# Inputs of the next pair made during the scan: two state-space layers and two token layers on one core

## The chip, the core and the metric

The kernel runs on one core of a Trainium2 chip. A core has five engines that run beside each other, each through its own list of instructions in order: TensorE (PE in the profile, with its weight loads as PEld), VectorE (DVE), ScalarE (ACT), GpSimd (POOL) and SyncE (SP, which here issues the DMA transfers). They wait for each other by semaphores. Operands lie in SBUF, results of TensorE in the eight banks of PSUM. The metric is the device time in microseconds (us) from start to end of the program.

## What is computed

The input x is four images of 64 x 64 places with 96 channels. Two layers of a two-dimensional selective scan follow each other, then two layers of linear attention and a quantised feed-forward net on the tokens. Of a scan layer, the part that matters here is

```
x   = x + layer(groupnorm(x))
xz  = einsum('bhwc,ec->bhwe', x, in_proj_w)          # 96 -> 2 * 192
xp, z = split(xz, 2)
xc  = silu(depthwise 3 x 3 convolution of xp + conv_b)
xs  = xc in four orders: rows, columns, and both from the end
x_dbl -> dts, B, C                                    # 6 + 16 + 16 rows
delta = softplus(dts @ dt_projs_w + bias)
h_t = exp(delta_t * A) * h_(t-1) + delta_t * u_t * B_t   # 16 states a channel
y_t = sum over states of C_t * h_t,  + D * u_t
y   = layernorm(sum of the four orders) * silu(z)
out = einsum('bhwd,cd->bhwc', y, out_proj_w)
```

## The kernel before

Two images make a pair, so there are four units in the order layer 0 pair 0, layer 0 pair 1, layer 1 pair 0, layer 1 pair 1. The 192 channels of a pair's two images fill three tiles of 128 rows: tile 0 and 1 hold 128 channels of one image each, tile 2 the remaining 64 of both. `u[0..2]` hold the inputs of the scan, 128 x 4096 each, in SBUF.

For each unit `between_scans` (L107) runs a stage, and then `scan.run()` the scan. The stage interleaves two generators: `scan_outputs` (L249) of the unit before, and `scan_inputs` (L122) of the unit to come. `scan_inputs` measures the group norm (`measure`, L174), projects 512 places at a time into padded images in SBUF (`project`, L198), writes silu(z) to DRAM (`zg`), and convolves: `conv_product` (L147) by nine matrix products with diagonal weights on TensorE, `conv_chain` (L158) by nine multiply-adds on VectorE. Here the order on an engine is the scheduler's. `scan_outputs` works in 16 groups of 256 places: load `zt`, `xr` and the sums `ys`; layer norm, transposition, product with `zt`, projection `po`, addition and store.

The scan (`PairScan.scan`, L458) is written out by hand: `InOrder` (L56) keeps the compute engines to the order of the program. Its 48 steps are (direction k, chunk of 1024 places, tile j), and a step is eight groups of two states, named by `n0`, the first of the two. For each state VectorE runs a first-order recurrence over 1024 places (`h`). Its two inputs are da = exp(delta A) from ScalarE and b = delta u B. The strings `OWN` and `SHARED` (L45) say who makes b for each state: V is VectorE, from B spread by TensorE with a selector `sel`; A is ScalarE (`outer`, L512) and a transposition by TensorE; G is GpSimd (`start_dbu`, L541). The result or its factor stands in `bp`, of which there are two. GpSimd multiplies h by C (`cb`, spread by DMA from DRAM); three groups later (LAG) TensorE turns the product to time order and adds it up in `yp`. `bp` takes four banks, `yp` two; `m0` and `m1` of one bank each serve two further pieces of work: `discretise` (L421), which makes delta, du and dut of the step to come, and `project` (L375), which makes B, C and dt of the chunk to come. Both are generators that `drive` (L481) takes on at named places; a value after `yield` is the n0 (for `project` with the tile or half ahead of it) at which the next part is to be issued.

After the last scan `token_layers` (L860) takes the outputs of the last unit together with the attention of the first images.

Of the kernel before, what the change touches and what calls it, by code (L numbers as in the profile page):

```python
# [44 lines left out]
OWN, SHARED = "VAVAVAAGVAVAVAVA", "VGVAVAVGVAVGVAVV"  # L45
# [39 lines left out]
class ScanLayer:  # L85


    def __init__(self, tc, pw, dram, x_src, w, n):
# [5 lines left out]

        self.zg = [dram.tile([3, 128, L], F32, name=f"zg{n}{pr}") for pr in range(NB // 2)]
# [11 lines left out]
def between_scans(tc, cst, ident, half, u, before, scan, after):  # L107


    with ExitStack() as stage:  # L110
        ins = scan_inputs(tc, stage, cst, ident, half, u, scan, *after)
        if before is not None:
            pp = stage.enter_context(tc.tile_pool(name="c_ps", bufs=2, space=PSUM))
            outs = scan_outputs(tc, stage, ident, half, *before, pp)
            for _ in outs:
                for _ in range(2):
                    next(ins, None)
        for _ in ins:
            pass


def scan_inputs(tc, stage, cst, ident, half, u, scan, layer, pr):  # L122


    nc = tc.nc
    par, zg, x_src = layer.par, layer.zg[pr], layer.x_src
    pa = stage.enter_context(tc.tile_pool(name="a", bufs=1))
    p2 = stage.enter_context(tc.tile_pool(name="a2", bufs=3))
    pp = stage.enter_context(tc.tile_pool(name="a_ps", bufs=5, space=PSUM))

    wi = pa.tile([C, 2, 2 * DI], F32, name="wi")
    nc.sync.dma_start(out=wi, in_=layer.w["wi"].rearrange("i c d -> c i d"))

    diag = pa.tile([128, 9, 128], F32, name="diag")
    for tap in range(9):
        nc.gpsimd.tensor_scalar(diag[:, tap], ident, par[:, 0, P_CONV + tap : P_CONV + tap + 1], None, ALU.mult)

    imgs = []
    for j in range(3):
        img = pa.tile([128, HW + 2, HW + 2], F32, name=f"img{j}", tag=f"img{j}")  # L140
        nc.gpsimd.memset(img[:, 0], 0.0)
        nc.gpsimd.memset(img[:, HW + 1], 0.0)
        nc.gpsimd.memset(img[:, 1 : HW + 1, 0:1], 0.0)
        nc.gpsimd.memset(img[:, 1 : HW + 1, HW + 1 : HW + 2], 0.0)
        imgs.append(img)

    def conv_product(j, c):  # L147

        ps = pp.tile([128, 8, HW], F32, name="cps", tag="mm")
        for tap in range(9):  # L150
            dy, dx = divmod(tap, 3)
            v = imgs[j][:, c + dy : c + dy + 8, dx : dx + HW]
            nc.tensor.matmul(ps, diag[:, tap], v, start=(tap == 0), stop=(tap == 8))
        nc.scalar.activation(
            u[j][:, HW * c : HW * (c + 8)], ps.rearrange("p h w -> p (h w)"), AF.Silu, bias=par[:, 0, P_CB : P_CB + 1]
        )

    def conv_chain(j, c):  # L158

        s, cols = j // 2, slice(HW * c, HW * (c + 16))  # L160
        to = u[j][:, cols].rearrange("p (h w) -> p h w", w=HW)
        for tap in range(9):
            dy, dx = divmod(tap, 3)
            v = imgs[j][:, c + dy : c + dy + 16, dx : dx + HW]
            weight = par[:, s, P_CONV + tap : P_CONV + tap + 1]
            if tap == 0:
                nc.vector.tensor_scalar(to, v, weight, par[:, s, P_CB : P_CB + 1], ALU.mult, ALU.add)
            else:
                nc.vector.scalar_tensor_tensor(to, v, weight, to, ALU.mult, ALU.add)
        nc.scalar.activation(u[j][:, cols], u[j][:, cols], AF.Silu)  # L170

    norms = []

    def measure(i):  # L174

        stats = p2.tile([C, 8, 6], F32, name="stats")
        for g in range(8):
            xt = p2.tile([C, 512], F32, name="xt", bufs=4)
            nc.sync.dma_start(out=xt, in_=x_src[2 * pr + i, :, 512 * g : 512 * g + 512])
            nc.vector.bn_stats(stats[:, g], xt)  # L180
            if g % 2:
                yield
        mv = p2.tile([C, 2], F32, name="mv")
        nc.vector.bn_aggr(mv, stats.rearrange("c g s -> c (g s)"))

        gm = pp.tile([C, 1], F32, name="gm", tag="mm")
        nc.tensor.matmul(gm, cst["group"], mv[:, 0:1], start=True, stop=True)
        mean = p2.tile([C, 1], F32, name="mean")
        nc.vector.tensor_copy(mean, gm)
        dev = p2.tile([C, 1], F32, name="dev")  # L190
        nc.vector.tensor_tensor(dev, mv[:, 0:1], mean, ALU.subtract)
        spread = p2.tile([C, 1], F32, name="spread")
        nc.vector.scalar_tensor_tensor(spread, dev, dev, mv[:, 1:2], ALU.mult, ALU.add)
        gv = pp.tile([C, 1], F32, name="gv", tag="mm")
        nc.tensor.matmul(gv, cst["group"], spread, start=True, stop=True)
        norms.append((mean, rstd_of(nc, p2, gv, [C, 1], "gn", half[:C, 0:1])))

    def project(i, c):  # L198


        mine, other = slice(D1 * i, D1 * i + D1), slice(D1 - D1 * i, 128 - D1 * i)
        cols, rows = slice(512 * c, 512 * c + 512), slice(1 + 8 * c, 9 + 8 * c)
        xn = p2.tile([C, 512], F32, name="xn")
        nc.sync.dma_start(out=xn, in_=x_src[2 * pr + i, :, cols])
        nc.vector.tensor_scalar(xn, xn, *norms[i], ALU.subtract, ALU.mult)
        pss = []
        for q in range(3):
            ps = pp.tile([128, 8, HW], F32, name=f"ips{q}", tag="mm")
            nc.tensor.matmul(ps, wi[:, i, 128 * q : 128 * q + 128], xn, start=True, stop=True)
            pss.append(ps)  # L210
        nc.scalar.copy(imgs[i][:, rows, 1 : HW + 1], pss[0])
        nc.scalar.copy(imgs[2][mine, rows, 1 : HW + 1], pss[1][mine])
        zs = p2.tile([128, 2, 512], F32, name="zs", bufs=2)
        flat = [ps.rearrange("p h w -> p (h w)") for ps in pss]
        nc.scalar.activation(zs[other, 0], flat[1][other], AF.Silu)
        nc.scalar.activation(zs[:, 1], flat[2], AF.Silu)
        nc.sync.dma_start(out=zg[i, :, cols], in_=zs[:, 1])
        nc.sync.dma_start(out=zg[2, mine, cols], in_=zs[other, 0])

    for i in range(2):  # L220
        yield from measure(i)
    for c in range(8):
        project(0, c)
        if c % 2:
            yield

    for c in range(8):
        project(1, c)
        if c == 2:
            conv_chain(0, 0)  # L230
        elif c == 5:
            conv_chain(2, 0)
        if c % 2:
            yield
    conv_product(1, 0)
    conv_product(1, 8)
    beginnings = scan.begin(nc, pp)
    for n in range(2, 8):
        conv_product(*((1, 8 * n) if n < 6 else (0, 8 * n)))
        for _ in range(4):  # L240
            next(beginnings, None)
        yield
        conv_chain(*((0, 16), (0, 32), (2, 16), (2, 32), (2, 48), (1, 48))[n - 2])
        yield
    for _ in beginnings:
        pass


def scan_outputs(tc, stage, ident, half, layer, pr, pp, turned="pt", summed="po"):  # L249
# [3 lines left out]
    p2 = stage.enter_context(tc.tile_pool(name="c2", bufs=3 if layer.last and pr else 2))  # L253
# [3 lines left out]
    for g in range(NT // 2):  # L257
# [25 lines left out]
        for t in range(2):  # L283
            for i in range(2):
                cols = slice(DI * i, DI * i + DI)
                nc.scalar.activation(
                    ys[:, t, cols], ys[:, t, cols], AF.Identity, bias=shift[:, t, i : i + 1], scale=rs[:, t, i : i + 1]
                )

        gt = p2.tile([128, 3, 2, 128], F32, name="gt")  # L290
        for t in range(2):
            pt = pp.tile([128, 3, 128], F32, name="pt", tag=turned)
            for j, first in enumerate((0, 256, 128)):
                nc.tensor.transpose(pt[:, j], ys[:, t, first : first + 128], ident)
            for s, js in ((0, slice(0, 2)), (1, slice(2, 3))):
                nc.scalar.activation(
                    gt[:, js, t],
                    pt[:, js],
                    AF.Identity,
                    bias=par[:, s, P_NB : P_NB + 1],  # L300
                    scale=par[:, s, P_NW : P_NW + 1],
                )
        nc.vector.tensor_tensor(gt, gt, zt.rearrange("p j (t q) -> p j t q", q=128), ALU.mult)
# [37 lines left out]
class PairScan:  # L341
# [112 lines left out]
    def run(self):  # L454
        with ExitStack() as stage:
            self.scan(stage, InOrder(self.tc))
# [495 lines left out]
def constants():  # L952
# [6 lines left out]
    for n in range(NS):  # L959
        for i in range(2):  # L960
            sel[:, i, n, n, i] = 1
# [101 lines left out]
```

## Time and profile before

| what | us |
|---|---|
| median of three runs | 10648.89 |
| lowest and highest | 10646.76, 10650.05 |
| the profiled execution | 10664.13 |
| its span | 10662.4 |
| the four scans, first to last VectorE scan operation | 2295.4, 2295.8, 2293.4, 2300.3 |
| from start to the first scan | 151.2 |
| from scan to scan | 226.7, 225.6, 237.8 |
| from the last scan to the end | 635.7 |

The page of the profile gives for each engine its busy time, then the span in 40 slices with the busy share of each in tenths, and groups of like instructions: line and engine, what is written and read, how many, then busy time, mean of one in ns, and the idle time of the engine just ahead of them with what ended it. Instructions that the scan issues all have the line of the helper (L71), so they are told apart by the names of their tiles. A product of two float32 operands shows as two passes on PE.

### The profile page before, as it was taken

To read this page: it belongs to the slowest core of one execution; us is meant where nothing else is said; L and a number is where in the kernel's file an instruction comes from. 1 tells how busy PE (TensorE), PEld (TensorE's weight loads), DVE (VectorE), ACT (ScalarE), POOL (GpSimd) and SP (SyncE) were. 2 spreads that over 40 slices of the span, in tenths; PEclk is the share of its full clock that TensorE was granted. 3 is DMA by queue.
4 is the path that set the end of the run, shared out by engine and by line. 5 is a ranking of instruction groups with operands and counts; after the bars stand their busy time and mean duration, and the time that the engine had idled before them with its cause. 6 is when DMAs were issued, how large, how long until landed. Compare 5 with 4: busy or idle time off the path is not lost. (4 is left out here: it accounts for less than half of the span.)

```text
span 10662.4 us, 142477 instructions
## 1 busy us (share of the span) xinstructions
PE 8056.0 (76%) x47648; PEld 5958.1 (56%) x47648; DVE 9606.8 (90%) x6874; ACT 8773.7 (82%) x18779; POOL 9021.4 (85%) x5298
## 2 busy tenths in 40 slices
PE   7777777777777777776877777777777777777666
PEld 4555555554555555554455555555455555555554
DVE  8999999997999999998899999999699999999755
ACT  6888888885888888886788888888598888888666
POOL 4999999992899999996599999999299999999645
PEclk9888898988888898998989889898888889899887
DMA  4677777775677777777567777777577777777710
GB/s 146 208 212 217 218 220 218 219 219 156 203 213 212 218 220 220 217 219 206 162 209 215 213 219 221 221 217 219 147 207 210 207 219 218 219 217 220 198 34 24
DMA packets 908758, 2126.70 MB, mean 199 GB/s; under 512 B 331094, under 2 KB 640664, under 8 KB 710296
## 3 DMA queue, kind: packets, MB, share of 16 engines
q1 hardware_dynamic: 908024, 2117.59, 69.3%
q8 instruction: 378, 6.19, 0.3%
q14 instruction: 356, 2.92, 0.1%
HBM read 1955.85 MB, written 161.48 MB: 199 GB/s over the span
## 5 line engine op out<-in xcount | busy, mean ns | idle before, releaser
L71 POOL TENSOR_TENSOR h<-h,cb 128x1024 f32<-128x1024 f32 x3072 | 7198.3, 2367 | 236.1 <-issue 68.6
L71 DVE TENSOR_TENSOR_SCAN h<-da,last,bp 128x1024 f32<-128x1024 f32 x2064 | 4736.5, 2335 | 142.0 <-PE bp L71 21.9
L71 ACT ACTIVATE x<-dut,bt 128x128 f32<-128x128 f32 x12288 | 3509.7, 378 | 1.6 <-PE bp L71 1.5
L71 PE MATMUL yp<-ident,h 128*128 128x128 f32 x24576 | 3365.5, 297 | 10.9 <-POOL h L71 10.9
L71 PEld LDWEIGHTS yp<-ident,h 128*128 128x128 f32 x24576 | 3191.8, 157 | 126.0 <-issue 74.0
L71 ACT ACTIVATE da<-delta,amat 128x1024 f32<-128x1024 f32 x2752 | 3076.3, 1147 | 95.7 <-DVE h L71 94.6
L71 PE MATMUL bp<-ident,x 128*128 128x128 f32 x10240 | 1672.5, 315 | 1292.8 <-DVE h L71 949.4
L71 PEld LDWEIGHTS bp<-ident,x 128*128 128x128 f32 x10240 | 1353.6, 162 | 1856.2 <-ACT x L71 1011.7
L71 DVE TENSOR_TENSOR bp<-du,bp 128x1024 f32<-128x1024 f32 x1472 | 1780.9, 1214 | 271.4 <-PE bp L71 269.6
L71 DVE TENSOR_TENSOR_SCAN h<-da,bp 128x1024 f32<-128x1024 f32 x688 | 1537.7, 2275 | 53.7 <-ACT da L71 12.9
L71 PE MATMUL bp<-bparts,sel 96*128 96x512 bf16 x2944 | 923.1, 399 | 755.2 <-DVE h L71 736.2
L71 PEld LDWEIGHTS <-sel 96*128 96x128 bf16 x2944 | 226.9, 100 | 1551.1 <-DVE h L71 1032.5
L71 ACT ACTIVATE bp<-delta,amat 128x1024 f32<-128x1024 f32 x320 | 358.2, 1119 | 520.1 <-DVE h L71 518.6
L71 POOL TENSOR_TENSOR dbu<-du,bb 128x1024 f32<-128x1024 f32 x320 | 755.4, 2361 | 0.0
L71 POOL COPY last<-h 128x2 f32<-128x2 f32 x1152 | 218.5, 190 | 490.0 <-DVE h L71 487.8
L71 DVE TENSOR_TENSOR_SCAN h<-bp,last,dbu 128x1024 f32<-128x1024 f32 x240 | 558.8, 2329 | 18.2 <-POOL dbu L71 17.1
L81 POOL TENSOR_TENSOR ln_rs<-ln_ve,half 128x4 f32<-128x4 f32 x64 | 84.8, 1325 | 546.6 <-DVE ln_ve L79 452.2
L71 PE MATMUL xps<-u,wx 128*76 128x512 f32 x720 | 532.7, 825 | 0.0
L71 ACT ACT_TABLE_LOAD x380 | 487.5, 1283 | 25.1 <-DMA x<-xo 18.3
L71 POOL TENSOR_TENSOR du<-delta,u 128x1024 f32<-128x1024 f32 x188 | 497.1, 2644 | 0.0
L71 PE MATMUL dps<-cdt,wdt 12*128 12x512 f32 x752 | 434.7, 658 | 0.0
L71 ACT COPY ysum<-yp 128x1024 f32<-128x1024 f32 x192 | 194.4, 1013 | 289.9 <-PE yp L71 289.8
(156 smaller groups left out, 6339.7 us busy)
## 6 DMA issues: line engine op xcount, KB each, us to landing
cb<-crow SPq DMA_DIRECT2D x1024, 1024.0 KB
cb<-crow SPq DMA_DIRECT2D x1024, 512.0 KB
bb<-crow SPq DMA_DIRECT2D x384, 256.0 KB
bb<-crow SPq DMA_DIRECT2D x128, 512.0 KB
y<-ysum SPq DMA_DIRECT2D x192, 256.0 KB
kept<-y SPq DMA_DIRECT2D x160, 256.0 KB
y<-ysum SPq DMA_DIRECT2D x64, 512.0 KB
zt<-zg SPq DMA_DIRECT2D x64, 384.0 KB
```

The lines of the kernel that those rows point to most:

```text
L71: return self.tc.keep_in_program_order(getattr(self.engine, op)(*args, **kwargs))
L81: nc.gpsimd.tensor_tensor(rs, ve, half, ALU.pow)
```

## The change

The inputs of the next unit are made while a scan runs. `first_inputs` is the old `scan_inputs` for the first unit alone, with eight PSUM banks, and it also measures the norm of images 2 and 3. For the later units an object `InputsAhead` holds a list of small jobs. A projection job is one product of 128 x 512; a convolution piece of 128 x 512 is two jobs, of five and four taps, and its input is read back from DRAM (`xi`). Each job writes the bank `m0` or `m1` between the uses by `discretise` and `project`; ScalarE copies the result out two states later, and SyncE stores it (`xi`, `zg` or `conv`). Projections, norms and convolutions no longer touch `u`.

The stage between then loads `conv` into `u`, applies silu there (`take`), and runs `scan_outputs`. z is stored without silu, which `scan_outputs` applies to `zt`; `scan_outputs` also takes the statistics for the norm of the next layer from what it has just made, and half of the layer norm's scaling moves to VectorE, except in the last unit. `discretise` is issued earlier. To make room in SBUF the selector shrinks to an identity that is read with stride 0 (`both` holds it written out for tile 2), GpSimd's b is written over its input, and the skip shares a buffer with `kept`. One G in `SHARED` moves from state 11 to state 13.

```
-OWN, SHARED = "VAVAVAAGVAVAVAVA", "VGVAVAVGVAVGVAVV"
+OWN, SHARED = "VAVAVAAGVAVAVAVA", "VGVAVAVGVAVAVGVV"
...
+class InputsAhead:
...
+        projections = [[("in", i, c, q) for q in range(3)] for i in range(2) for c in range(8)]
+        conv = [[[("conv", j, c, h) for h in range(2)] for c in range(8)] for j in range(3)]
+        pieces = projections[:8] + conv[0] + projections[8:] + conv[1] + [[("diag",)]] + conv[2]
...
+    def load(self, nc, n):
...
+        self.given[n] = given = self.pb.tile([128, 10 * HW], F32, name="given", bufs=2)
...
+            nc.sync.dma_start(out=to, in_=self.layer.xi[self.pr][i, :, HW * lo : HW * hi])
...
+    def prepare(self, nc, n):
...
+            nc.scalar.activation(xn, xn, AF.Identity, bias=shift, scale=scale)
...
+    def start(self, nc, pm, tag, more):
...
+        kind, i, c, part = job
+        if kind == "conv" and part == 0 and not more:
+            return
+        self.jobs.pop(0)
+        if part == 0:
+            self.load(nc, n + 1)
...
+            ps = pm.tile([128, 512], F32, name="aps", tag=tag)
+            nc.tensor.matmul(ps, self.wi[:, 128 * part : 128 * part + 128], self.given[n][:C, :512], start=True, stop=True)
...
+            def close():
+                out = self.pb.tile([128, 512], F32, name="bout", bufs=2)
+                nc.scalar.copy(out, ps)
...
+        if part == 0:
+            self.open = pm.tile([128, 8, HW], F32, name="bps", tag=tag)
...
+        taps = (4, 0, 1, 2, 3, 5, 6, 7, 8)
+        for tap in taps[:5] if part == 0 else taps[5:]:
...
+            nc.tensor.matmul(ps[:, h, w], self.diag[:, tap], v, start=(tap == 4), stop=(tap == 8))
...
+        def close():
+            out = self.pb.tile([128, 512], F32, name="bout", bufs=2)
...
+            nc.scalar.activation(out, ps.rearrange("p h w -> p (h w)"), AF.Identity, bias=bias)
+            nc.sync.dma_start(out=layer.conv[pr][i, :, 512 * c : 512 * c + 512], in_=out)
+            self.prepare(nc, n + 1)
...
+def between_scans(tc, cst, ident, half, pn, u, before, scan, layer, pr):
...
+        def take(n):
+            for j in range(3):
+                cols = slice(T * n, T * n + T)
+                nc.sync.dma_start(out=u[j][:, cols], in_=layer.conv[pr][j, :, cols])
+                nc.scalar.activation(u[j][:, cols], u[j][:, cols], AF.Silu)
+
+        take(0)
+        outs = scan_outputs(tc, stage, cst, ident, half, pn, *before, pp)
+        beginnings = scan.begin(nc, pb)
+        for g, _ in enumerate(outs):
+            if g % 4 == 1 and g > 4:
+                take(g // 4)
...
+                if alone and i:
+                    nc.vector.tensor_scalar(v, v, scale, bias, ALU.mult, ALU.add)
+                else:
+                    nc.scalar.activation(v, v, AF.Identity, bias=bias, scale=scale)
...
+        nc.scalar.activation(zt, zt, AF.Silu)
         nc.vector.tensor_tensor(gt, gt, zt.rearrange("p j (t q) -> p j t q", q=128), ALU.mult)
...
+            for i in range(2):
+                norms[i].take(nc, xo[:, i])
...
+        yield 0
         for hf, cols in enumerate(halves):
-            yield 2 * hf
             ps = pm.tile([128, 512], F32, name="dps", tag=tags[hf])
...
-        yield 4
+        yield 2
         for ps, cols in zip(pss, halves):
             nc.scalar.activation(delta[:, cols], ps, AF.Softplus, bias=bias)
-        yield 6
+        yield 4
...
-            yield 10 + 2 * hf
+            yield 6 + 2 * hf
...
-            yield 12 + 2 * hf
+            yield 8 + 2 * hf
...
-                    out[i] = p2.tile([128, T], F32, name="dbu", bufs=1)
-                    nc.gpsimd.tensor_tensor(out[i], made[groups[g][0]][1], bbs.pop((g, i))[:, 0], ALU.mult)
+                    out[i] = bbs.pop((g, i))[:, 0]
+                    nc.gpsimd.tensor_tensor(out[i], made[groups[g][0]][1], out[i], ALU.mult)
...
+        def drive_ahead(place):
+
+            j, n0 = place
+            if later is None:
+                return
+            if n0 in (4, 6, 12, 14):
+                later.finish()
+            if n0 in (10, 12) or j < 2 and n0 in (2, 4):
+                later.start(nc, pm, "m0" if n0 >= 10 else "m1", n0 in (2, 10))
```

`drive_ahead` is called once a group: at n0 = 14 right after `drive(projecting)` ahead of the next group's inputs, and in the other groups after `drive(discretising)` and ahead of `drive(projecting)`.

## The prediction

> **What bounds the kernel now.** I read the page first, for the engines' shares, then busy time by stage, then the waits of one scan, then a timeline of a few microseconds, then the costliest groups between two scans.
>
> ```profile
> span 10662.4 us, 142477 instructions
> PE 8056.0 (76%) x47648; PEld 5958.1 (56%) x47648; DVE 9606.8 (90%) x6874; ACT 8773.7 (82%) x18779; POOL 9021.4 (85%) x5298
> ...
> DVE  8999999997999999998899999999699999999755
> ...
> 151.20:2446.60 2295.40, 1748.38 (x10646) 1326.04 (x10646) 2173.62 (x1150) 1989.59 (x4270) 2153.42 (x1197) 0.89 0.75 215
> 2446.60:2673.40 226.80, 176.24 (x530) 88.13 (x530) 155.76 (x312) 116.97 (x225) 33.13 (x41) 0.88 0.53 146
> ```
>
> The last two rows are a scan and the stage after it (columns: window, length, PE, PEld, DVE, ACT, POOL busy, clock, DMA share, GB/s). A scan fills 2173.6 of its 2295.4 us on DVE and 2153.4 on POOL: only 122 us of DVE idle are to be had there, and whatever makes DVE wait lengthens the kernel. The stages between last scan operation and first of the next take 226.7, 225.6 and 237.8 us, 690 together, with no engine full: PE 176, DVE 156.
>
> What makes DVE wait in a scan (us, times, longest):
>
> ```profile
> DVE bp L71 <- PE bp L71: 56.8, 73, 1.7
> ...
> PE dups L71 <- ACT dut L71: 19.8, 27, 1.5
> ```
>
> PE, though 76% busy, is what DVE waits for. A timeline of two groups shows why:
>
> ```profile
> 1044.37 1.21 DVE L71 TENSOR_TENSOR bp<-du,bp 128x1024 f32<-128x1024 f32 x1
> ...
> 1045.50 1.91 PE L71 MATMUL yp<-ident,h 128*128 128x128 f32 x16
> 1047.24 0.60 PE L71 MATMUL dups<-ident,du 128*128 128x128 f32 x4
> 1047.68 1.88 PE L71 MATMUL xps<-u,wx 128*76 128x512 f32 x2
> 1049.38 0.61 PE L71 MATMUL bp<-bparts,sel 96*128 96x512 bf16 x2
> 1050.18 1.21 DVE L71 TENSOR_TENSOR bp<-du,bp 128x1024 f32<-128x1024 f32 x1
> ...
> 1054.44 0.66 PE L71 MATMUL dups<-ident,du 128*128 128x128 f32 x4 [1.22 <-ACT dut L71]
> 1054.93 1.88 PE L71 MATMUL xps<-u,wx 128*76 128x512 f32 x2
> 1056.63 0.61 PE L71 MATMUL bp<-bparts,sel 96*128 96x512 bf16 x2
> ```
>
> A group takes DVE 5.8 us (one product 1.21, two scans 4.6). Both `bp` buffers are in use, so PE can't run ahead. After DVE begins a group, PE is done with `bp` and `yp` at 1047.41, 3.0 us in; the next `bp` must start about 5.0 us in. So 2.0 us of a group are free on PE. In the first group `dups` and `xps` (2.3 us) just fit: DVE goes on at 1050.18, 5.81 later. In the second PE also waited 1.22 us for ACT, and the next `bp` came at 1056.63, 6.45 in: DVE lost 1.18 us.
>
> **The skill.** "Perfetto Trace Analysis", Optimization Strategy, says that regimes with different limits may gain from being interleaved, which fits the two window rows; its Identifying the Most-Contended Engine warns that PE's busy time is no measure of PE's room, and the timeline agrees: 2.0 us a group, not 24%, and only at one place. "ScalarE: Activation LUTs", What ACT_TABLE_LOAD costs, gives 1283 ns for a load; the page here has the same mean, 1283. "DMA: Bandwidth & Descriptors", Measured, has 341 GB/s for 1 MB transfers; the trace moves 215 in a scan, with 331094 packets under 512 B, so I use the trace's.
>
> **Part 1: the stage between.** Removed: `project`, convolution and the norm's first pass. In their place 12 loads of ready convolutions and 12 Silu of 128x1024. What stays per group of outputs is little to compute and much to move: `zt` 0.39 MB, `xr` 0.20, `ys` 0.39, `xo` 0.20, 1.17 in all; 16 groups 18.7 MB, with `u` 6.3 MB: 25 MB. At 215 GB/s 116 us. DVE for a group:
>
> ```profile
> L278 DVE BATCH_NORM_STATS2 ystats<-ys 128x6 f32<-128x192 f32 x64 | 20.1, 342 | 17.2 <-DMA ys<-y 17.2
> L303 DVE TENSOR_TENSOR gt<-gt,zt 128x768 f32<-128x768 f32 x16 | 15.3, 954 | 11.6 <-ACT gt L296 11.6
> L312 DVE TENSOR_TENSOR xo<-xr,po 96x512 f32<-96x512 f32 x16 | 10.8, 678 | 13.9 <-PE po L310 13.9
> ```
>
> (instructions, busy, mean ns, idle before). 20.1+10.0 (aggregates)+15.3+10.8+5.2 (small ones), plus the two normalising products that move over from ACT (2x16 at about 0.3) and 32 statistics of `xo` (about 0.4): 84 us. ACT: 15.2+32.8 us of its present work, 16 Silu of 128x768 (0.9 by the 1.06 of 128x1024) and 12.7 for `u`: 75. So DMA is next in line, not an engine. The first `ystats` ran 16.4 us after the last scan operation (sum, store, load) and a group lasts 12 us from there. 16.4 + 15 groups at 6.6-7 + 12 + 4 to the first scan operation = 133 us; 120 if transfers are quicker, 150 if they stay as in the tail, where 16 groups take 7.7 us each. Gain 690 - 3x133 = 291 us.
>
> **Part 2: jobs in the first three scans.** Each scan gets 48 projection jobs and 24 convolution pieces, a piece cut into 5 and 4 taps in successive slots. The prices stand in the stage between: 144 passes of `cps` 64.1 us, two passes a tap, so 0.89 a tap; 96 passes of `ips` 45.3, 0.94 a projection. One stage has 216 taps and 48 projections: 216x0.89 + 48x0.94 = 237 us more for PE, from 1748 to 1985 of 2295: that fits on average and not in place. A piece is 4.45 and then 3.56 us against 2.0 free. The slots are the groups that begin with state 2, 4, 10 or 12 for tiles 0 and 1, and 10 or 12 for tile 2. In 10 and 12 of tiles 0 and 1 PE has `xps` behind the job, 1.5 us on average (180 passes 133.3). DVE then loses 2.45+1.55 = 4.0 us a piece in 2,4 and 3.95+3.05 = 7.0 in 10,12; in tile 2 4.0, of which POOL's backlog there (its own 49.4 us of a 49.9 us step) hides about 1. Mix 2:2:1: 5.0 a piece, 120 us a scan. ACT's part: in the group of state 10 the bank m0 is given free by the copy of `dut`, at 2 the bank m1 by the softplus, and PE stands behind these as in the second group above: 1.2 us on 14 pieces, 17 us. Projections fit except beside `xps` or behind ACT: 0.5 on average, 24 us. Some of this falls where DVE waits already (122 us a scan): minus 20. Sum 140 a scan, 420. Bounds: 84 (3.5 a piece, nothing else) to 200 (ACT late at every slot).
>
> ACT gains 48x0.59 + 24x0.6 + 16x0.5 = 51 us of 2295, to 89%; DMA 30 MB on 494. SP issues a store behind ACT's copy and a load behind PE's last tap; `cb` loads queue behind them, two groups ahead of POOL: no cost.
>
> **Part 3: discretise earlier, in all four scans.** Both `dps` stand in the group of state 0, 1.16 us more (188 passes 108.8), where PE already runs late after tile 2: DVE lost 1.32 there in the step that I read. Loss up to 1.16 in 32 of 48 steps, 37 us; less what later waits take back: 25, bounds 0 and 37. The `dups` pair moves from 10,12 to 6,8 with its wait on ACT: even. SHARED's G moves from 11 to 13 and the skip shares a buffer: DVE's 8 us of waiting for `dbu` go, 10 a scan gained, bounds 0 and 15. `dbu` in place and the broadcast selector keep their counts: nothing, unless weight loads slow down (100 ns now; twice that still fits). Sum 4x(25-10) = +60.
>
> **Part 4: ends.** Two more images measured in the first stage: 16 statistics at 0.67, 10.5 us of DVE, half beside PE's convolutions: +8. Silu of `zt` in the tail: 16x0.8 of ACT, and two table switches: +8 of the 636.
>
> Sum: -291 + 420 + 60 + 16 = +205. The profiled execution (10664.1 with a span of 10662.4) lies 15 us above the median 10648.9; against the median that is 10855.
>
> **Rivals.**
> *PE hides the jobs* (faster). For it: PE idles 547 us of a scan and 237 are asked. Against: the 1.18 us above, lost to only 1.22 of delay. If a piece costs 2 us, not 5, a scan grows by 55: -291 + 165 - 25 (part 3 at its lower side) + 16 = -135, 10515. It decides the sign where the first three scans grow by less than 87 us each, part 3's 15 among them: (291-16-15)/3.
> *The stage between is held by DMA and chain latency* at 185 us: gain 135. For it: small packets, and the wait on `ys`. Against: 16.4 us of first latency only. 11010.
> *ACT is the bound*: closing copies, softplus and ysum before every slot's matmul, 240 us a scan. For it: 87% busy now. Against: it runs up to a group ahead. -291 + 720 + 60 + 16: 11155.
> That the inputs aren't made in the scan I exclude: the order of PE's instructions has the jobs between `yp` and `bp`.
>
> **Numbers.** My forecast 0.45, PE hides 0.20, DMA 0.20, ACT 0.15. The forecast's own range is 10740 to 11000 (jobs 100 to 190 a scan). With the others, 10560 to 11100. A measurement here tells 0.2% (21 us) from nothing. Faster 0.17, within 0.05, slower 0.78.
>
> **What would show it.** Stages between of about 133 us, with DMA near 215 GB/s; scans 1 to 3 some 155 us longer than now and the fourth some 15; DVE's wait for PE `bp` in them near 200 us, at groups after slots 2, 4, 10, 12; `aps` and `bps` waiting for ACT. I am wrong if the first scans grow by under 87 us, or if the stages stay above 170.

## The result, and the profile after

The changed kernel took 11289.0 us in the median of four runs (11272.9 to 11299.7), the kernel before 10647.8 beside it: a ratio of 1.0602, 95% interval 1.0583 to 1.0620. It is 641 us slower where 205 were forecast, and lies above the stated range. From the page of the profile:

```profile
span 11297.6 us, 144738 instructions
PE 8561.7 (76%) x48512; PEld 6262.4 (55%) x48512; DVE 9408.9 (83%) x6763; ACT 8810.1 (78%) x18808; POOL 9034.9 (80%) x5289
...
DVE  7878888987888878989787888898779899988755
```

DVE has 198 us less to do than before and is 635 us longer at it; no engine is fuller than 83%. The new time is waiting. By stage (window, length, PE, PEld, DVE, ACT, POOL busy with instructions, clock, DMA share, GB/s): the stage ahead of the second scan, the third scan, which makes inputs for the unit to come, and the fourth, which has nothing to make:

```profile
2703.60:2845.00 141.40, 83.57 (x296) 52.49 (x294) 79.75 (x274) 77.61 (x140) 19.94 (x20) 0.72 0.64 178
...
5532.10:8076.20 2544.10, 1982.92 (x11171) 1438.44 (x11172) 2182.17 (x1150) 2037.22 (x4359) 2164.45 (x1206) 0.89 0.70 207
...
8233.40:10646.40 2413.00, 1789.62 (x10642) 1363.74 (x10643) 2177.45 (x1150) 1988.31 (x4270) 2158.31 (x1197) 0.88 0.70 205
```

With the ends of VectorE's scan operations for borders, the two profiled executions compare as follows. The fourth scan separates two costs: it has all edits of the scan, and no job.

| stretch | before | after | difference |
|---|---|---|---|
| start to first scan | 151.2 | 159.9 | +8.7 |
| scans 1 to 3, each | 2295.4, 2295.8, 2293.4 | 2543.7, 2544.9, 2544.1 | |
| scan 4 | 2300.3 | 2413.0 | |
| all four: edits of the scan, 2413.0 less the mean of 2296.2 | | | +467 |
| scans 1 to 3: jobs, 2544.2 less 2413.0 | | | +394 |
| stages between | 226.7, 225.6, 237.8 | 141.4, 142.2, 157.2 | -249 |
| last scan to end of the span | 636.1 | 651.2 | +15.1 |

These add up to 635 us, as the spans differ (the 635.7 us to the end given further up were read to 10662.0, not to 10662.4). What the stages between gained, the jobs alone more than took back, and the larger loss has nothing to do with jobs. In the fourth scan (us waited, times, longest):

```profile
DVE bp L72 <- PE bp L72: 177.7, 115, 3.6
...
PE dups L72 <- ACT dut L72: 138.5, 47, 4.8
...
PE yp L72 <- ACT ysum L72: 53.6, 35, 4.4
```

and in the second scan of the kernel before:

```profile
DVE bp L71 <- PE bp L71: 65.7, 84, 1.7
...
PE dups L71 <- ACT dut L71: 23.1, 30, 1.5
```

VectorE still waits for TensorE's `bp` and for little else, but now 178 us of a scan, not 66. TensorE waits for ScalarE's copy of `dut` in all 47 steps that have one to come, 139 us in place of 23. The timeline of one such place, in the fourth scan, in the groups of state 8 and 10 (weight loads are among the lines left out):

```profile
9168.41 0.60 PE L72 MATMUL bp<-bparts,sel 96*128 96x512 bf16 x2
...
9168.84 1.04 PE L72 MATMUL bp<-ident,x 128*128 128x128 f32 x8
9169.04 1.23 DVE L72 TENSOR_TENSOR bp<-du,bp 128x1024 f32<-128x1024 f32 x1 [1.07 <-PE bp L72]
...
9169.72 1.91 PE L72 MATMUL yp<-ident,h 128*128 128x128 f32 x16
9170.05 2.44 ACT L72 ACTIVATE x<-dut,bt 128x128 f32<-128x128 f32 x8
...
9172.39 1.13 ACT L72 ACTIVATE da<-delta,amat 128x1024 f32<-128x1024 f32 x1
...
9173.43 0.56 ACT L72 COPY dut<-dups 128x512 f32<-128x512 f32 x1
...
9174.04 0.66 PE L72 MATMUL dups<-ident,du 128*128 128x128 f32 x4 [2.42 <-ACT dut L72]
...
9174.54 1.88 PE L72 MATMUL xps<-u,wx 128*76 128x512 f32 x2
...
9176.24 1.03 PE L72 MATMUL bp<-bparts,sel 96*128 96x512 bf16 x2
...
9177.31 1.23 DVE L72 TENSOR_TENSOR bp<-du,bp 128x1024 f32<-128x1024 f32 x1 [2.35 <-PE bp L72]
```

TensorE has finished `yp` at 9171.6. Its next instruction turns the second half of `du` into the bank of the first, and ScalarE copies the first half out at 9173.43, only after the `x` and `da` of the group to come. `dups`, `xps` and the `bp` for which VectorE waits all stand behind that copy: VectorE begins the group 8.3 us after the one before, 2.35 of them idle.

### The profile page after: what moved, and what is told of

The parts are those of the page before. It is cut to its first block, busy times and chain, and to the rows that moved or that the text cites. A ratio compares the mean times of both kernels' runs of the same rounds, so it can differ in the third digit from the quotient of the medians.

```text
span 11297.6 us, 144738 instructions
## 1 busy us (share of the span) xinstructions
PE 8561.7 (76%) x48512; PEld 6262.4 (55%) x48512; DVE 9408.9 (83%) x6763; ACT 8810.1 (78%) x18808; POOL 9034.9 (80%) x5289
## 5 line engine op out<-in xcount | busy, mean ns | idle before, releaser
L72 PE MATMUL bp<-ident,x 128*128 128x128 f32 x10240 | 1625.2, 310 | 731.2 <-DVE h L72 517.1
L72 POOL TENSOR_TENSOR bb<-du,bb 128x1024 f32<-128x1024 f32 x320 | 755.4, 2361 | 0.0
L72 PE MATMUL bp<-bparts,sel 96*128 96x512 bf16 x1792 | 584.5, 410 | 208.6 <-DVE h L72 198.4
L72 PE MATMUL dups<-ident,du 128*128 128x128 f32 x1504 | 256.9, 297 | 596.7 <-ACT dut L72 523.6
L72 PE MATMUL bp<-bparts,both 96*128 96x512 bf16 x1152 | 404.6, 440 | 373.9 <-DVE h L72 368.3
L72 PE MATMUL bps<-given,bdiag 128*128 128x504 f32 (+3 forms) x1296 | 580.6, 594 | 27.5 <-ACT delta L72 26.1
L72 PEld LDWEIGHTS <-sel 96*128 96x128 bf16 x1792 | 158.1, 103 | 790.6 <-issue 429.3
L72 DVE TENSOR_TENSOR_SCAN h<-bp,last,bb 128x1024 f32<-128x1024 f32 x240 | 557.9, 2325 | 3.1 <-POOL bb L72 3.1
L72 PEld LDWEIGHTS dups<-ident,du 128*128 128x128 f32 x1504 | 174.3, 148 | 656.3 <-ACT dut L72 567.5
```

The lines of the kernel that those rows point to most:

```text
L72: return self.tc.keep_in_program_order(getattr(self.engine, op)(*args, **kwargs))
```

## The experiments

Each stood beside runs of the kernel before on the same chip (10642 to 10643 us in the median). "Growth by jobs" is the mean of scans 1 to 3 less the fourth.

| run | us | ratio, interval | scans 1 to 3 | scan 4 | growth by jobs |
|---|---|---|---|---|---|
| changed kernel | 11289.0 | 1.0602 (1.0583 to 1.0620) | 2544 | 2413 | 131 |
| e1_times_only | 11166.7 | 1.0488 (1.0472 to 1.0503) | 2419 | 2419 | none made |
| e2_small_edits | 10690.9 | 1.0042 (1.0027 to 1.0057) | 2302 | 2305 | none made |
| e3_copy_first | 10936.4 | 1.0275 (1.0260 to 1.0291) | 2456 | 2332 | 124 |
| e5_thirds | 10782.8 | 1.0133 (1.0116 to 1.0149) | 2415 | 2304 | 111 |
| e8_one_tap | 11034.5 | 1.0369 (1.0353 to 1.0384) | 2457 | 2420 | 37 |
| e7_small_early | 10561.1 | 0.9923 (0.9908 to 0.9938) | 2273 | 2270 | none made |
| e6_thirds_early | 10561.8 | 0.9927 (0.9910 to 0.9943) | 2354 | 2249 | 106 |
| e9_no_jobs | 10472.5 | 0.9844 (0.9830 to 0.9859) | 2253 | 2254 | none made |
| e10_halves | 10685.5 | 1.0037 (1.0024 to 1.0049) | 2401 | 2253 | 148 |

**Only the earlier places of discretise, on the kernel before.**

```
+        yield 0
         for hf, cols in enumerate(halves):
-            yield 2 * hf
...
-        yield 4
+        yield 2
...
-        yield 6
+        yield 4
...
-            yield 10 + 2 * hf
+            yield 6 + 2 * hf
...
-            yield 12 + 2 * hf
+            yield 8 + 2 * hf
```

From the top: both `dps` (after one yield now), the softplus, `du`, `dups` and the copies to `dut`.

> The kernel before with one part of the change: discretise's pieces issued at the earlier places, nothing else. Theory A (the earlier dups wait for ACT's copy of dut, in every step): the fourth scan of the changed kernel, which has no jobs, is 113 us longer than before, so each of four scans grows by about 113: 10648 + 450 = 11100 us, and TensorE's wait of dups for dut grows from about 22 to about 135 us a scan. Theory B (the other small edits of the scan, selector, shared buffer and the moved G, make the 113): within 60 us of before. The prediction's own term would give 4 x 25 = +100.

It took 11166.7 us: 524 more than before, each scan some 122 longer. That is as much as the fourth scan of the changed kernel loses, and five times the prediction's term. Its waits in the second scan:

```profile
DVE bp L71 <- PE bp L71: 197.2, 116, 4.0
...
PE dups L71 <- ACT dut L71: 85.4, 32, 3.1
```

VectorE's wait is where the changed kernel has it; `dups` waits 85 us of a scan, less than the 135 expected and nearly four times the 23 of before.

**Only the small edits of the scan, on the kernel before** (selector, b over its input, shared buffer, `SHARED` with a G at 13).

> The kernel before with the other edits inside the scan: selector read with stride 0 and written out for tile 2, GpSimd's b over its input, skip and kept in one buffer, one G from state 11 to 13. Theory A: near before, by the prediction's term 40 us faster, 10610 (10590 to 10660). Theory B: slower by 300 to 450, 11000 to 11100.

10690.9 us: 48 slower. Theory B is out as the cause, but the prediction's 40 us of gain are not there either. The waits name a new one, in the second scan:

```profile
PE dups L72 <- ACT dut L72: 65.4, 43, 3.6
...
DVE bp L72 <- PE bp L72: 41.7, 66, 1.6
DVE rest L72 <- ACT parts L72: 40.9, 15, 3.7
```

In tile 2 the group of state 10 now has state 11 made by ScalarE. ScalarE comes later to the casts of the new chunk's B (`parts`), and VectorE's small subtraction `rest`, queued between two scans, holds VectorE for 2.7 us a time. The first line shows something else: TensorE waits 65 us for `dut` here, at the old places, and VectorE waits less for `bp` than before. So the time that TensorE waits is not yet time lost; that depends on what stands behind the wait.

**ScalarE's copy first, in the changed kernel.**

```
+            if n0 in (8, 10):
+                drive(discretising, n0)
             if n0 == NS - NG:
                 drive(discretising, n0)
...
             if g + 1 < len(groups):
                 ahead, cb_next, dbu_next = start_ahead(g + 1), start_cb(g + 1), start_dbu(g + 1)
```

> The changed kernel with discretise's parts of the groups of state 8 and 10 issued ahead of the next group's da and x, so that ACT copies dut before it makes these. TensorE's order is the same. Theory A (PE stands behind ACT's late copy): the wait of dups for dut falls below 40 us a scan, the fourth scan falls from 2413 to 2300 to 2340, the first three by as much, the whole to about 10900. Theory C (PE's own load in these groups, kept, dups and xps, makes the loss, not the wait): the fourth scan stays above 2380, the whole above 11150.

10936.4 us, 353 less. The same work in the same order on TensorE, with the copy ahead of `da` and `x` on ScalarE, takes most of the loss away. The fourth scan's window and waits, and one group of state 6 in tile 2 of that scan:

```profile
7959.00:10290.70 2331.70, 1758.44 (x10641) 1335.72 (x10642) 2172.93 (x1150) 1986.30 (x4270) 2152.56 (x1197) 0.89 0.70 212
...
DVE bp L72 <- PE bp L72: 105.6, 70, 4.0
...
PE yp L72 <- ACT ysum L72: 54.1, 37, 4.1
```

```profile
8660.95 3.78 PE L72 MATMUL yp<-kept,ident 128*128 128x512 f32 x4 [3.34 <-ACT ysum L72]
...
8668.81 1.23 DVE L72 TENSOR_TENSOR bp<-du,bp 128x1024 f32<-128x1024 f32 x1 [3.95 <-PE bp L72]
```

The wait of `dups` for `dut` is gone. Where the time went shows when a scan is taken apart by groups. The table gives the mean time in us from VectorE's first operation of a group to its first of the next, in the fourth scan. A scan has 32 such groups in tiles 0 and 1 and 16 in tile 2.

| kernel | state 6, tiles 0, 1 | state 6, tile 2 | state 8, tiles 0, 1 | state 8, tile 2 | state 12, tiles 0, 1 |
|---|---|---|---|---|---|
| before | 4.55 | 5.84 | 5.82 | 6.08 | 6.27 |
| e1_times_only | 5.15 | 9.02 | 8.34 | 6.10 | 5.93 |
| changed kernel | 5.15 | 8.77 | 8.09 | 7.60 | 6.01 |
| e3_copy_first | 5.15 | 8.99 | 5.88 | 6.75 | 5.81 |

At state 8, where the second half of `dups` now stands, the changed kernel loses 97 us a scan, and the copy ahead gives 84 of them back. At state 6, where the first half stands, it loses 66, most of it in tile 2, and the copy gives nothing back. The 35 us that are left over the 2296 of before are these, less what other groups gained. In the group shown, TensorE first waits 3.34 us for `ysum`, whose copy frees `yp`, and `dups` and the turning of B (`btps`) come behind that, before the next `bp`. The run with the places alone has this wait too, 52 us in its second scan; the run with the small edits has 20. Before, `ysum` followed the softplus directly on ScalarE; now the softplus stands a group earlier, with `da` and `x` of another group in between. No run separates these.

**Jobs of one tap.**

```
-        for tap in taps[:5] if part == 0 else taps[5:]:
+        for tap in taps[:1] if part == 0 else taps[8:]:
```

> The changed kernel with one tap in each half of a convolution piece in place of five and four: it leaves out seven ninths of the convolution made during the scans; slots, banks, copies, loads and stores stay. Theory A (what a job costs is the length of its products beside the 2.0 us free): 24 x 7 x 0.89 = 150 us of PE fall away, and the first three scans grow over the fourth by 20 to 50 us in place of 131: total near 11000. Theory E (a job costs by its waits for the bank and by ACT's copies, not by its products): growth stays above 90, total above 11150.

11034.5 us, with seven taps of nine left out. The third scan and the fourth:

```profile
5347.10:7809.80 2462.70, 1870.26 (x10834) 1389.71 (x10835) 2179.36 (x1150) 2037.39 (x4359) 2161.88 (x1206) 0.88 0.72 214
7963.70:10383.50 2419.80, 1798.55 (x10642) 1372.42 (x10643) 2177.97 (x1150) 1988.77 (x4270) 2156.85 (x1197) 0.87 0.68 204
```

ScalarE, GpSimd and the transfers do what they do in the changed kernel, and the jobs cost 37 us a scan in place of 131. So 94 of the 131 us are the length of the products; borrowed banks, copies, loads and stores together with the projections and the two taps that stay are within the 37.

**Old places, other slots, pieces in thirds.** Discretise as before; jobs in m0 only, at the groups of state 4, 6 and 8.

```
-            if n0 in (10, 12) or j < 2 and n0 in (2, 4):
-                later.start(nc, pm, "m0" if n0 >= 10 else "m1", n0 in (2, 10))
+            if n0 in (4, 6, 8):
+                later.start(nc, pm, "m0", n0 == 4)
...
-        for tap in taps[:5] if part == 0 else taps[5:]:
+        for tap in taps[3 * part : 3 * part + 3]:
```

> The changed kernel with discretise at the places of before, and the jobs in the bank m0 alone in the groups of state 4, 6 and 8, where discretise leaves it free; a convolution piece in three jobs of three taps, results copied out ahead of the next group's da and x. By the prediction's price a job of three taps (2.67 us) overruns the 2.0 us free on PE by 0.7, 72 of them 50 us a scan, projections nothing: first three scans 2300 + 50 - 10, fourth 2290, stages between 141, 141, 157: 10648 - 250 + 120 - 10 + 24 = 10530 us, faster than both. Theory D (jobs cost what they cost in the changed kernel wherever they stand, 131 us a scan): 10820.

10782.8 us, 253 more than I expected. The fourth scan is back at 2304, but the jobs cost 111 us a scan, not 50. Taken apart by groups, these are 37 us at state 4, 36 at 6, 7 at 8 and 24 at 12: a third of a piece, with the projections that share its slots, costs about 1.5 us at states 4 and 6, not the 0.7 that followed from the 2.0 us read in one group of state 10. And the subtraction's wait is there again, 28 to 41 us a scan.

**ScalarE's casts first, without jobs.** On the run with the small edits, `rest` gets a place of its own behind VectorE's scans, and the casts of B go ahead of `da` and `x`.

```
+            if (j, n0) == (2, 8):
+                drive(projecting, (j, n0))
             if g + 1 < len(groups):
...
         nc.scalar.copy(parts[:, :, 0], ps)
+        yield 2, 9
         nc.vector.tensor_tensor(rest, ps, parts[:, :, 0], ALU.subtract)
```

> The kernel before with the other small edits of the scan, and ACT's two casts of the new chunk's B issued ahead of the next group's da and x, with VectorE's subtraction (rest) behind its scans. In the run without this, DVE stood 27 to 41 us a scan before rest, for ACT, in the group of state 10 of tile 2 (8.7 us in place of 6.6), since the moved G makes that group one with ten states' worth of ACT work. If that wait is the reason why the small edits cost rather than gain: 10690 - 4 x 35 = 10550, faster than before. If another wait takes its place: 10650 or more.

10561.1 us, as expected: the small edits lost 48 us through that one wait, and without it gain 81. `rest` is no longer among VectorE's waits in the second scan, where it waits 53.5 us for `bp`.

**Thirds, with casts and first copy of dut ahead.** The same edit on the run with thirds, and `drive(discretising)` ahead of the next inputs at state 12 as well.

> The run with convolutions in thirds, with ACT's casts of B and its first copy of dut issued ahead of the next group's da and x. Theory A: rest's wait (28 to 41 us a scan) and the wait of dups for dut (about 22) go: 10783 - 4 x 45 = 10600, a little faster than before. If PE's length of work in the groups of state 6 and 8 sets the pace anyway: 10700 or more.

10561.8 us: faster than both kernels. Third and fourth scan:

```profile
5142.20:7494.70 2352.50, 1925.46 (x11166) 1373.90 (x11167) 2176.89 (x1150) 2038.41 (x4359) 2160.92 (x1206) 0.92 0.75 224
...
7645.80:9894.30 2248.50, 1723.20 (x10638) 1285.97 (x10639) 2169.92 (x1150) 1985.10 (x4270) 2150.05 (x1197) 0.91 0.73 220
```

Without jobs a scan now takes 2249 us, 48 less than in the kernel before; jobs still add 106.

**The same without jobs**, on the kernel before.

> The kernel before with the small edits of the scan and both early groups of ACT work (casts of B, first copy of dut): no jobs, the stage between as before. The run with thirds has the same scan without jobs in its fourth: 2248 us. Four such scans and the stages of before: 147 + 4 x 2250 + 680 + 636 - 14 = about 10450, 110 us faster than the run with thirds. If instead the jobs' stage and scan come out even, 10560.

10472.5 us, the fastest of all, 1.6% under the kernel before. One scan and the stage after it:

```profile
5102.00:7353.00 2251.00, 1726.92 (x10638) 1291.55 (x10639) 2170.08 (x1150) 1985.10 (x4270) 2150.57 (x1197) 0.91 0.74 220
7353.00:7587.70 234.70, 188.92 (x732) 110.27 (x730) 147.21 (x294) 123.77 (x241) 33.33 (x41) 0.84 0.50 143
```

It makes no inputs ahead, and beats the run with jobs by 89 us in the medians, by 64 between the profiled executions (10473.3 and 10537.2). There the jobs make the four scans 297 us longer (9310.9 against 9014.1) and both ends 19, and the stages between gain 252 (680.3 less 428.6).

From e7_small_early this run differs only in the copy of `dut` ahead at state 12, the old place. That is worth 89 us, 19 a scan, though TensorE waited 64 us a scan for the copy there. At the new place in the changed kernel the same move gave 81 a scan.

**Halves again**, in the slots of state 4 and 6, on the run with thirds and early copies.

> The run with thirds and early copies, with the pieces in halves of five and four taps in the groups of state 4 and 6 again. Theory A (PE's work over the room of its group is what DVE loses): 4.45 - 2.0 and 3.56 - about 1.1 make 4.9 us a piece, against 4.4 measured with thirds; scans some 10 to 20 us longer, total 10580 to 10620. Theory F (smaller jobs hide markedly better): 10650 or more.

10685.5 us: this missed. The growth is 148 us a scan, 6.2 a piece, where I had worked out 4.9; thirds cost 4.4. Smaller jobs do hide better than my sum of overruns has it.

## Why the prediction was wrong

| step, as the prediction put it | predicted | measured |
|---|---|---|
| stages between: 133 us each, -291 | -291 | -249 |
| jobs: "Sum 140 a scan, 420" | +420 | +394 |
| discretise earlier and small edits: 4x(25-10) | +60 | +467 |
| both ends | +16 | +24 |

The step that failed is one sentence in part 3: "The `dups` pair moves from 10,12 to 6,8 with its wait on ACT: even." It was not even. The groups of state 6 and 8, where the pair went, grew by 66 and 97 us a scan; those of state 10 and 12, where it had stood, shrank by 11 and 21. At state 8 the cause is shown: with ScalarE's copy ahead 84 of the 97 us come back, and 353 us of the whole. At state 6 it stays open between the wait for `ysum` and the work that stands behind it. All moves of discretise together lose 524 us in the run that has nothing else; both `dps` in one group, for which the prediction had 25 us a scan, are not where it lost them: there the groups of state 0 and 2 change by +14 and -13.

The prediction had the mechanism in hand, from the second group of its own timeline, and priced it for the jobs; for the moved pair it took the old price over without reading how late ScalarE is in those groups. In tiles 0 and 1 the copy that the second half of `dups` waits for began 3.1 us into its group at the old place, state 12. At state 8 it began 4.9 us in, in the changed kernel and in the run with the places alone, and 2.3 us in with the copy ahead (means of the fourth scan). Its bounds for that part, 0 to 37 us a scan for `dps` and nothing for `dups`, then kept the range too narrow; even its own rival of 11155 us lay outside the range.

The gain of 10 us a scan from the small edits was wrong in sign: 48 us lost in all, through a wait that the prediction didn't name, VectorE's subtraction behind ScalarE's casts. In the changed kernel that wait is only 12 us of the fourth scan.

The price of the jobs held as a sum: 140 forecast, 131 measured, in the groups that have the slots (43 and 21 us at state 2 and 4, 46 and 21 at 10 and 12). The one-tap run bears out that it is mostly the length of the products beside a small room, not the borrowed banks. That the sums agree so well is in part luck: of its 120 us for the pieces the prediction's mix had 38 at 2 and 4 and 82 at 10 and 12, and the two pairs cost about the same. Two later expectations built on "2.0 us a group" missed, one by 253 us in total.

The stages between were 8, 9 and 24 us longer than 133. The first moved the 25 MB that were worked out, at 178 GB/s with both ends in it; its first statistics ran 20.2 us after the last scan operation, not 16.4. In the trace VectorE goes to them straight from `du` of the coming scan, for which it had waited 5.61 us on ScalarE's delta. In the next stage it waits another 0.24 us for `ys` itself, so those loads, which now stand behind a load of `u`, came hardly sooner. Neither was tried. The third stage was the longest already before, 237.8 us against 226, and the prediction priced all three alike.

Of the rivals, "PE hides the jobs" is refuted by 131 us a scan. "ACT is the bound" named the right engine for the wrong reason: ScalarE was busy 82% of the fourth scan, and most of the time was lost by the place of one 0.56 us copy in its order. "DMA" is refuted by the 141 us.

## What to carry to other kernels

Where several engines run lists in a fixed order, a step that is moved has to be priced at its new place: read there how far behind each engine is that it waits for and what stands behind the wait, not what the wait cost at the old one. A short copy that frees a buffer for TensorE belongs ahead of the long work that nobody waits for yet; here one such move was worth 353 us, more than the 249 that the shorter stages gained. Average idle time is no room: ask how long the engine may be late in one turn of the loop, and cut filler to that. Even in thirds the jobs cost the scans more, 297 us, than the shorter stages gained, 252.

## What had not been expected of the hardware

After TensorE's wait of 2.42 us its products ran slower a little later: in the timeline above a `bp` pair of 0.60 us took 1.03. The windows of that wait and of the slow pair (columns as before, the clock third from the end):

```profile
9171.60:9174.00 2.40, 0.03 (x1) 0.00 (x0) 2.40 (x2) 2.40 (x7) 2.32 (x3) 1.00 0.73 140
9175.20:9178.40 3.20, 3.20 (x11) 1.81 (x10) 1.09 (x1) 3.20 (x10) 3.12 (x4) 0.50 0.44 182
```

The granted clock fell from 1.00 to 0.50 after the wait, from 9175.11 to 9178.52. Over the whole of that execution such a pair took 0.61 us at a clock of 1.00 and 1.03 at 0.50 (medians of 1177 and 156 pairs). The Trainium skill, "TensorE: Matmul & The Clock Gate", What's actually happening, says that the clock follows how busy the engine has been of late, and the trace agrees. So here a wait cost more than its own length: VectorE, waiting for that pair, began about 0.4 us later for it. The clock can't be the main cause of the lost time, as its mean in the fourth scan was 0.88 against 0.89 in the kernel before; what part of the loss runs by way of it no run separates.
